# An attention layer over pairs of blocks: correction and factor over the whole width, num a pair further ahead

## The chip, the cores and the metric

The kernel runs on one core of a Trainium2 chip, as one launch. The metric is the device time of one execution in microseconds (us). Engines are named as in the profile: PE is TensorE's matmul, PEld its weight load, DVE is VectorE, ACT is ScalarE, POOL is GpSimd, and SP is SyncE, which here only issues DMAs. L1519 means line 1519 of the kernel before.

## The reference

The input is a matrix x of 2708 rows and 128 columns and a weighted adjacency matrix adj of 2708 by 2708. Four layers follow each other, each one x = layernorm(x + layer(x, adj)). The first is a graph convolution with an adaptive nearest-neighbour term, the third and the fourth are plain graph convolutions. The change lies in the second layer, an attention layer:

```python
XW = jnp.matmul(X, W)
s_col = jnp.matmul(XW, a[0, :f])
s_row = jnp.matmul(XW, a[0, f:])
Z1 = jax.nn.leaky_relu(s_row[:, None] + s_col[None, :], negative_slope=0.01)
den = jnp.exp(Z1)
num = jnp.matmul(A, den)
att = jnp.where(num != 0, den / jnp.where(num != 0, num, 1.0), 0.0)
H = jnp.matmul(A, jnp.matmul(att, XW))
```

So there is one product of 2708 by 2708 by 2708 (num), an elementwise quotient, and two products with narrow matrices.

## The kernel before

The kernel does not compute num as a full product. den(i, j) is exp of a leaky relu of a sum, and so one of two exponentials, according to the sign of s_row(i) + s_col(j). The columns j are sorted by s_col and cut into 44 blocks of 62 (BJ). From one block to the next num changes only by the rows of adj whose sign changes inside the block, at most 126 (KC) of them. So the rows of num for one block are a product of a small weight matrix lw with those gathered rows of adj, plus two rows that carry the sums at the block's beginning. Four blocks (CH) make a chain: the end of one block gives the carried rows of the next.

The steps of the block stage (`block_layer`) are pairs of blocks: 22 pairs (NQ), once for each half h of the columns (HALF = 1354), so 44 steps (h, q). A block takes 64 of the 128 partitions: two rows of carried sums and 62 of num. The 1354 columns are cut into two pieces, "wide" (1024) and "narrow" (330), since num lies in PSUM: the wide piece has two buffers, the narrow one has one, and the sum hacc takes the rest. A step has these parts:

- `load` (L1397, L1403): two gathers of up to 126 rows of adj, issued by POOL, and two copies of the carried rows, issued by SP, into one of three strips of `ring`.
- `find_num` (L1519): the matmuls num <- ring, lw. A piece of 512 or 330 columns has two, one for each block, on 64 columns of PE each, and they show as four records since data are f32.
- `find_inv` (`invert`, L1351 and L1354): ACT's Ln and then Exp(-...) of num, the inverse, in SBUF. For the two carried rows of a block the scale and bias in `plain` make it the inverse of 1.
- `mix_1` (L1361): DVE's err = inverse times num. Its two carried rows are what the next block of the chain needs, and `keep` (L1534) copies them into `carry` with four DMAs from SP where the chain goes on.
- `mix_2` (L1365), here called the correction: a Newton step on the inverse with err. `mix_3` (L1368), here called the factor: the numerator of the quotient, max(gb, g_inv) times the inverse, in place.
- `add_up` (L1376): the matmuls hacc <- inverse, xws, which sum att transposed times XW over the steps of a half.

The order on every engine is written out by hand (`manual_schedule` over all five): what the loop issues first goes first in that engine's queue. Step i of the loop issues the load of step i+2, a fetch of one tile of xws on POOL (L987, the first eight steps), num narrow of i, num wide of i+1, hacc of i-1, the inverses in the same order as the nums, ACT's scaling of xws (L1566, first half only), and then on DVE err, correction and factor of step i, each as wide and narrow. Ahead of the loop stand the loads 0 and 1 and num and inverse of step 0 wide. At the first step of the second half ACT copies the first half's sum (L1568). Behind the last step PE transposes ten tiles (L1587), then does the last hacc. A `POOL` power for the next layer (L253, dinv) and its first loads are queued by their own place in the program. The arm used when a block has more than 126 rows (`dense_layer`) does not run with these inputs.

Of the kernel before, what the change touches and what calls it, by code (L numbers as in the profile page):

```python
# [8 lines left out]
F32 = mybir.dt.float32  # L9
# [43 lines left out]
def kernel(  # L53
# [1294 lines left out]
    def invert(w, num, pool, bufs, sums=True):  # L1348
        inv = pool.tile([P, w], F32, tag=f"inv{w}", name="inv", bufs=bufs)
        if sums:  # L1350
            nc.scalar.activation(inv, num[:, :w], AF.Ln, scale=plain[:, 0:1], bias=plain[:, 1:2])  # L1351
        else:
            nc.scalar.activation(inv, num[:, :w], AF.Ln)
        nc.scalar.activation(inv, inv, AF.Exp, scale=-1.0)  # L1354
        return inv

    def mix_1(w, num, inv, pool):
        err = pool.tile([P, w], F32, tag=f"err{w}", name="err")  # L1360
        nc.vector.tensor_mul(err, inv, num[:, :w])  # L1361
        return err
# [50 lines left out]
    def dense_layer():  # L1413
# [3 lines left out]
        with (  # L1417
# [68 lines left out]
            for h in range(2):  # L1486
                hacc = dps.tile([P, 3 * CW], F32, tag="hacc", name="hacc")
                for q in range(NQ):
# [10 lines left out]
                    inv = invert(HALF, num, dense, 1, sums=False)  # L1499
                    mix_2(inv, mix_1(HALF, num, inv, dense))  # L1500
# [3 lines left out]
    def block_layer():  # L1504
        with (
# [17 lines left out]

            def find_inv(i, piece):
                invs[i, piece] = invert(pieces[piece][1], nums[i, piece], own, 3)

            def keep(i, piece, err):

                (h, q), (c0, w, _) = steps[i], pieces[piece]
                for n in range(2):  # L1530
                    b = block(2 * q + n) + 1
                    if b % CH:
                        o = h * HALF + c0
                        nc.sync.dma_start(  # L1534
                            carry[2 * b : 2 * b + 2, o : o + w], err[n * (BJ + 2) : n * (BJ + 2) + 2, :]
                        )

            def add(i):
# [3 lines left out]
                for piece, (c0, w, _) in pieces.items():  # L1542
                    add_up(w, q, invs[i, piece], haccs[h][:, c0 : c0 + w])

            engines = {nc.tensor, nc.vector, nc.scalar, nc.sync, nc.gpsimd}
            with tc.manual_schedule(engines={e.engine for e in engines}):
                load(0)
                load(1)
                late_q = list(range(SOON, NQ))
                find_num(0, "wide")  # L1550
                find_inv(0, "wide")
                for i, (h, q) in enumerate(steps):
                    if i + 2 < len(steps):
                        load(i + 2)
                    if late_q:
                        fetch_xw(xws, late_q.pop(0))
                    find_num(i, "narrow")
                    if i + 1 < len(steps):
                        find_num(i + 1, "wide")
                    if i:  # L1560
                        add(i - 1)
                    find_inv(i, "narrow")
                    if i + 1 < len(steps):
                        find_inv(i + 1, "wide")
# [4 lines left out]
                    if i + 1 < len(steps):  # L1569
                        errs = {}  # L1570
                        for piece, (c0, w, _) in pieces.items():
                            errs[piece] = mix_1(w, nums[i, piece], invs[i, piece], own)
                            keep(i, piece, errs[piece])
                        for piece in pieces:
                            mix_2(invs[i, piece], errs[piece])
                        for piece, (c0, w, _) in pieces.items():
                            mix_3(w, q, invs[i, piece], h * HALF + c0)
                    else:
                        for piece, (c0, w, _) in pieces.items():
                            mix_2(invs[i, piece], mix_1(w, nums[i, piece], invs[i, piece], own))  # L1580
                            mix_3(w, q, invs[i, piece], h * HALF + c0)
# [133 lines left out]
```

## Time and profile before

| what | us |
|---|---|
| runs of the kernel before: median of 3 | 1096.37 (1093.6 to 1104.44) |
| the profiled execution's own time | 1095.12 |
| its span, first to last instruction | 1093.3 |
| mean granted TensorE clock | 0.968 |

| engine | busy us | share of the span | instructions |
|---|---|---|---|
| PE | 1001.2 | 92% | 3691 |
| DVE | 641.2 | 59% | 1354 |
| ACT | 338.3 | 31% | 617 |
| POOL | 262.2 | 24% | 334 |

The block stage lies between 532 and 763 us of the span. Times in the views are counted from the span's start. In the chain of waits, each entry is what ended last, followed back from the end. In a timeline, a row gives start, time, engine, line, operation, tiles with the buffer numbers left out, and the count of instructions that were merged into it; in brackets stand the idle time ahead of it and what ended that. A matmul's end is modelled, so distances between PE's work are taken from start to start.

### The profile page before, as it was taken

Reading aid. Unit: us, or ns where it says so; the run is one execution under the profiler, and the core shown is the slowest. Engines: PE = TensorE matmul, PEld = TensorE weight load, DVE = VectorE, ACT = ScalarE, POOL = GpSimd, SP = SyncE. Lnnn points to the kernel's source line nnn. Section 1 sums busy time; section 2 is a strip of 40 time slices with the busy share of each in tenths; the row PEclk is TensorE's granted clock in tenths of the full one; section 3 lists DMA queues with packets and bytes.
Section 4 is the critical chain, followed back from the end, with each engine's and each line's share of the span. In section 5 each row is a group of like instructions: output and inputs, shape, how many; then the busy total and the mean of one; then the engine's idle time right before and its main releaser. Section 6 shows DMA issues by size and latency. Waiting matters only on the chain.

```text
span 1093.3 us, 11460 instructions
## 1 busy us (share of the span) xinstructions
PE 1001.2 (92%) x3691; PEld 483.3 (44%) x3691; DVE 641.2 (59%) x1354; ACT 338.3 (31%) x617; POOL 262.2 (24%) x334
## 2 busy tenths in 40 slices
PE   0798999999997898798799999999999999999996
PEld 0345544444443455643233333334444644565444
DVE  5983448999943477772498999998112112132122
ACT  0000125555401144612466776665001100011000
POOL 4000000000565564015584444430112100000000
PEclk9998999999998999699899999999999999999998
DMA  9999330000283556497545545555675875574752
GB/s 341 371 316 279 115 116 1 0 1 1 66 276 119 176 166 202 137 357 244 135 130 161 147 126 161 143 152 181 222 239 150 278 226 185 171 235 159 241 159 76
DMA packets 109380, 190.31 MB, mean 174 GB/s; under 512 B 13666, under 2 KB 46706, under 8 KB 109310
## 3 DMA queue, kind: packets, MB, share of 16 engines
q1 hardware_dynamic: 91408, 151.79, 42.6%
q0 software_dynamic: 17728, 37.62, 12.4%
q8 instruction: 31, 0.51, 0.2%
q14 instruction: 39, 0.32, 0.1%
q10 hardware_dynamic: 174, 0.08, 0.0%
HBM read 214.37 MB, written 4.16 MB: 200 GB/s over the span
## 4 chain that ended last, share of the span: by engine, by line
PE 79%; DVE 7%; DMA 6%; issue 4%; ACT 2%; POOL 1%; another core or an unknown queue 1%; SPq 1%; POOLq 0%; DVEq 0%; ACTq 0%
PE acc L204 32%; PE num L1519 9%; PE hacc L1376 9%; PE acc L647 8%; PE acc L428 7%; DMA res<-in_adjT 3%; PE acc L1270 3%; PE acc L637 2%; DMA got<-y_rows,where 1%; PE mis L285 1%; DVE where L650 1%; DMA part<-in_adjT 1%; DVE near L649 1%; DVE both L483 1%
## 5 line engine op out<-in xcount | busy, mean ns | idle before, releaser
L1397 POOL DMA_INDIRECT ring<-in_adjT,slot_i x88 | 96.2, 1093 | 116.4 <-PE num L1519 87.3
L1519 PE MATMUL num<-ring,lw 128*64 128x512 f32 (+1 forms) x528 | 114.8, 557 | 3.7 <-DVE err L1361 1.9
L1376 PE MATMUL hacc<-inv,xws 128*128 128x512 f32 (+1 forms) x264 | 111.7, 559 | 0.6 <-issue 0.3
L647 PE MATMUL acc<-zT,z 128*128 128x512 f32 (+4 forms) x264 | 108.6, 558 | 0.0
L1351 ACT ACTIVATE inv<-num,plain 128x1024 f32<-128x1024 f32 x88 | 80.6, 916 | 60.6 <-PE num L1519 35.8
L253 POOL TENSOR_TENSOR rstd<-rstd,minus_half 128x4 f32<-128x4 f32 (+1 forms) x18 | 17.3, 960 | 313.4 <-DVE rstd L252 313.4
L648 ACT COPY key<-acc 128x512 f32<-128x512 f32 (+3 forms) x132 | 70.2, 535 | 59.8 <-issue 29.8
L234 ACT COPY gb<-acc 128x512 f32<-128x512 f32 (+2 forms) x18 | 9.6, 535 | 251.0 <-PE acc L204 251.0
L1361 DVE TENSOR_TENSOR err<-inv,num 128x1024 f32<-128x1024 f32 x88 | 74.3, 853 | 20.1 <-ACT inv L1354 16.1
L204 PE MATMUL acc<-ring,y 128*128 128x512 f32 (+2 forms) x192 | 81.3, 554 | 0.5 <-POOL sim L584 0.5
L1376 PEld LDWEIGHTS hacc<-inv,xws 128*128 128x128 f32 x264 | 46.5, 189 | 77.6 <-issue 45.7
L677 POOL DMA_INDIRECT got<-y_rows,where x66 | 69.7, 1056 | 39.1 <-DVE near_sum L690 16.0
L204 PE MATMUL acc<-ring,xs 128*128 128x512 f32 (+2 forms) x192 | 77.2, 545 | 0.0
L1368 DVE SCALAR_TENSOR_TENSOR inv<-gb,g_inv,inv 128x1024 f32<-128x1024 f32 x88 | 77.0, 913 | 0.1
L204 PE MATMUL acc<-ring,carry 128*128 128x512 f32 (+2 forms) x192 | 74.5, 542 | 0.0
L204 PE MATMUL acc<-ring,m_rows 128*128 128x512 f32 (+2 forms) x192 | 74.3, 542 | 0.0
L1365 DVE SCALAR_TENSOR_TENSOR inv<-err,inv 128x1024 f32<-128x1024 f32 x88 | 72.3, 860 | 0.1
L647 PEld LDWEIGHTS acc<-zT,z 128*128 128x128 f32 (+1 forms) x264 | 47.5, 188 | 54.9 <-issue 49.4
L1354 ACT ACTIVATE inv<-inv 128x1024 f32<-128x1024 f32 x88 | 67.6, 768 | 2.8
L649 DVE MAX8 near<-key 128x8 f32<-128x2708 f32 (+1 forms) x22 | 65.5, 2978 | 3.9 <-ACT key L648 3.9
L575 POOL TENSOR_TENSOR slot_e<-near,sim 128x44 f32<-128x44 f32 (+2 forms) x3 | 0.7, 243 | 272.7 <-DVE d2inv L603 266.0
L650 DVE FIND_INDEX8 where<-near,key 128x8 uint32<-128x2708 f32 (+1 forms) x22 | 65.4, 2972 | 0.0
(357 smaller groups left out, 1351.6 us busy)
## 6 DMA issues: line engine op xcount, KB each, us to landing
ring<-in_adjT SPq DMA_DIRECT2D x86, 1024.0 KB
ring<-in_adjT SPq DMA_DIRECT2D x19, 768.0 KB
part<-in_adjT SPq DMA_DIRECT2D x12, 1024.0 KB
ring<-in_adjT SPq DMA_DIRECT2D x19, 552.0 KB
res<-in_adjT SPq DMA_DIRECT2D x4, 1280.0 KB
more<-in_adjT SPq DMA_DIRECT2D x4, 1024.0 KB
part<-in_adjT SPq DMA_DIRECT2D x3, 768.0 KB
part<-in_adjT SPq DMA_DIRECT2D x3, 552.0 KB
```

Source lines behind the costliest of these rows:

```text
L204: nc.tensor.matmul(accs[c][: lhsT.shape[-1], :w], lhsT=lhsT, rhs=src, start=start, stop=stop)
L428: nc.tensor.matmul(accs[c][:, : cw[c]], lhsT=y[:, i, :], rhs=src[:, : cw[c]], start=first, stop=last)
L647: nc.tensor.matmul(pks[c][:p, : cw[c]], lhsT=z2[:, :p], rhs=zT[:, cs], start=False, stop=True)
L649: nc.vector.max(near[:p, t, :], key[:p])
L650: nc.vector.max_index(where[:p, t, :], near[:p, t, :], key[:p])
L1351: nc.scalar.activation(inv, num[:, :w], AF.Ln, scale=plain[:, 0:1], bias=plain[:, 1:2])
L1361: nc.vector.tensor_mul(err, inv, num[:, :w])
L1365: nc.vector.scalar_tensor_tensor(inv, err, 2.0, inv, op0=ALU.subtract, op1=ALU.mult)
L1368: nc.vector.scalar_tensor_tensor(inv, gb[:, col : col + w], g_inv[:, q : q + 1], inv, op0=ALU.max, op1=ALU.mult)
L1376: nc.tensor.matmul(haccs[:, o:e], lhsT=xws[:, q, :], rhs=inv[:, o:e], start=(q == 0), stop=(q == NQ - 1))
L1397: nc.gpsimd.indirect_dma_start(out=rows[i][:KC, n, :], out_offset=None, in_=adj_half[:, :], in_offset=bass.IndirectOffsetOnAxis(ap=slot_i[ ...
L1519: nc.tensor.matmul(num[n * (BJ + 2) : (n + 1) * (BJ + 2), o:e], lhsT=lw[:, 2 * q + n, :], rhs=rows[i][:, n, c0 + o : c0 + e], start=True, ...
```

## The change

- `invert` writes into a tile that it is given. An inverse and an err are now one tile of 1354 columns for both pieces; `part` cuts out a piece.
- The correction and the factor take 1354 columns in one instruction instead of 1024 and 330, but for the last step. err, num and the inverse stay in two pieces.
- The factor of step i-1 is issued with step i, behind err of i and ahead of the correction of i, and hacc of i-1 behind it.
- num and inverse are a step further ahead: step i issues num narrow of i+1 and num wide of i+2, and the load of i+3. Ahead of the loop stand three loads, num and inverse of step 0 and of step 1 wide.
- There are four inverse buffers: three in `own`, and for every fourth step the second half of `mT`, which is free until the end of the stage.
- The copy of the first half's sum stands ahead of the wide inverse of step i+2, and behind the narrow one of i+1.
- Four kept-row DMAs are issued right behind err, ahead of the nums in the program.

The order of the instructions on each engine, as the program is built, is that of the code. On PE a round is num narrow (i+1), num wide (i+2), hacc (i-1); on DVE err wide, err narrow, factor (i-1), correction (i); on ACT inverse narrow (i+1), the scaling of xws, inverse wide (i+2); on SP two row copies of load i+3, four kept-row copies of i; on POOL two gathers of load i+3 and a fetch of xws.

```diff
-    def invert(w, num, pool, bufs, sums=True):
-        inv = pool.tile([P, w], F32, tag=f"inv{w}", name="inv", bufs=bufs)
+    def invert(inv, num, sums=True):
...
-    def mix_1(w, num, inv, pool):
-        err = pool.tile([P, w], F32, tag=f"err{w}", name="err")
-        nc.vector.tensor_mul(err, inv, num[:, :w])
-        return err
...
+            def part(v, piece):
+                c0, w, _ = pieces[piece]
+                return v[:, c0 : c0 + w]
+
             def find_inv(i, piece):
-                invs[i, piece] = invert(pieces[piece][1], nums[i, piece], own, 3)
+                if i not in invs:
+                    invs[i] = mT[:, HALF:] if i % 4 == 1 else own.tile([P, HALF], F32, tag="inv", name="inv", bufs=3)
+                invert(part(invs[i], piece), nums[i, piece])
...
+                end = len(steps)
+                late_q = list(range(SOON, NQ))
                 load(0)
                 load(1)
-                late_q = list(range(SOON, NQ))
-                find_num(0, "wide")
-                find_inv(0, "wide")
+                load(2)
+                for i, piece in ((0, "wide"), (0, "narrow"), (1, "wide")):
+                    find_num(i, piece)
+                    find_inv(i, piece)
                 for i, (h, q) in enumerate(steps):
-                    if i + 2 < len(steps):
-                        load(i + 2)
+                    if i + 3 < end:
+                        load(i + 3)
                     if late_q:
                         fetch_xw(xws, late_q.pop(0))
-                    find_num(i, "narrow")
-                    if i + 1 < len(steps):
-                        find_num(i + 1, "wide")
+                    err = own.tile([P, HALF], F32, tag="err", name="err")
+                    for piece in pieces:
+                        nc.vector.tensor_mul(part(err, piece), part(invs[i], piece), nums[i, piece])
+                        if i + 1 < end:
+                            keep(i, piece, err)
+                    if i + 1 < end:
+                        find_num(i + 1, "narrow")
+                    if i + 2 < end:
+                        find_num(i + 2, "wide")
                     if i:
+                        mix_3(HALF, steps[i - 1][1], invs[i - 1], steps[i - 1][0] * HALF)
                         add(i - 1)
-                    find_inv(i, "narrow")
-                    if i + 1 < len(steps):
-                        find_inv(i + 1, "wide")
+                    if i + 1 < end:
+                        mix_2(invs[i], err)
+                        find_inv(i + 1, "narrow")
                     if h == 0:
                         nc.scalar.mul(xws[:, q, :], xws[:, q, :], g_col[:, q : q + 1])
                     if (h, q) == (1, 0):
                         nc.scalar.copy(mT[:, :HALF], haccs[0][:, :HALF])
-                    if i + 1 < len(steps):
-                        errs = {}
-                        for piece, (c0, w, _) in pieces.items():
-                            errs[piece] = mix_1(w, nums[i, piece], invs[i, piece], own)
-                            keep(i, piece, errs[piece])
-                        for piece in pieces:
-                            mix_2(invs[i, piece], errs[piece])
-                        for piece, (c0, w, _) in pieces.items():
-                            mix_3(w, q, invs[i, piece], h * HALF + c0)
-                    else:
-                        for piece, (c0, w, _) in pieces.items():
-                            mix_2(invs[i, piece], mix_1(w, nums[i, piece], invs[i, piece], own))
-                            mix_3(w, q, invs[i, piece], h * HALF + c0)
+                    if i + 2 < end:
+                        find_inv(i + 2, "wide")
+                for piece, (c0, w, _) in pieces.items():
+                    mix_2(part(invs[end - 1], piece), part(err, piece))
+                    mix_3(w, q, part(invs[end - 1], piece), h * HALF + c0)
```

More of the change, by code (lines that the diff above doesn't have):

```diff
@@ L1346 @@
     more.close()
-    def invert(w, num, pool, bufs, sums=True):
-        inv = pool.tile([P, w], F32, tag=f"inv{w}", name="inv", bufs=bufs)
+    def invert(inv, num, sums=True):
         if sums:
-            nc.scalar.activation(inv, num[:, :w], AF.Ln, scale=plain[:, 0:1], bias=plain[:, 1:2])
+            nc.scalar.activation(inv, num, AF.Ln, scale=plain[:, 0:1], bias=plain[:, 1:2])
         else:
-            nc.scalar.activation(inv, num[:, :w], AF.Ln)
+            nc.scalar.activation(inv, num, AF.Ln)
         nc.scalar.activation(inv, inv, AF.Exp, scale=-1.0)
-        return inv
-    def mix_1(w, num, inv, pool):
-        err = pool.tile([P, w], F32, tag=f"err{w}", name="err")
-        nc.vector.tensor_mul(err, inv, num[:, :w])
-        return err
     def mix_2(inv, err):
@@ L1498, in dense_layer @@
                         nc.scalar.mul(xws[:, q, :], xws[:, q, :], g_col[:, q : q + 1])
-                    inv = invert(HALF, num, dense, 1, sums=False)
-                    mix_2(inv, mix_1(HALF, num, inv, dense))
+                    inv = dense.tile([P, HALF], F32, tag="inv", name="inv")
+                    err = dense.tile([P, HALF], F32, tag="err", name="err")
+                    invert(inv, num[:, :HALF], sums=False)
+                    nc.vector.tensor_mul(err, inv, num[:, :HALF])
+                    mix_2(inv, err)
                     mix_3(HALF, q, inv, h * HALF)
@@ L1534, in keep @@
                         nc.sync.dma_start(
-                            carry[2 * b : 2 * b + 2, o : o + w], err[n * (BJ + 2) : n * (BJ + 2) + 2, :]
+                            carry[2 * b : 2 * b + 2, o : o + w], part(err, piece)[n * (BJ + 2) : n * (BJ + 2) + 2, :]
                         )
@@ L1542, in add @@
                 for piece, (c0, w, _) in pieces.items():
-                    add_up(w, q, invs[i, piece], haccs[h][:, c0 : c0 + w])
+                    add_up(w, q, part(invs[i], piece), haccs[h][:, c0 : c0 + w])
             engines = {nc.tensor, nc.vector, nc.scalar, nc.sync, nc.gpsimd}
             with tc.manual_schedule(engines={e.engine for e in engines}):
+                end = len(steps)
+                late_q = list(range(SOON, NQ))
                 load(0)
                 load(1)
-                late_q = list(range(SOON, NQ))
-                find_num(0, "wide")
-                find_inv(0, "wide")
+                load(2)
+                for i, piece in ((0, "wide"), (0, "narrow"), (1, "wide")):
+                    find_num(i, piece)
+                    find_inv(i, piece)
                 for i, (h, q) in enumerate(steps):
-                    if i + 2 < len(steps):
-                        load(i + 2)
+                    if i + 3 < end:
+                        load(i + 3)
                     if late_q:
                         fetch_xw(xws, late_q.pop(0))
-                    find_num(i, "narrow")
-                    if i + 1 < len(steps):
-                        find_num(i + 1, "wide")
+                    err = own.tile([P, HALF], F32, tag="err", name="err")
[7 more added lines that the diff above has]
+                        find_num(i + 2, "wide")
                     if i:
+                        mix_3(HALF, steps[i - 1][1], invs[i - 1], steps[i - 1][0] * HALF)
                         add(i - 1)
-                    find_inv(i, "narrow")
-                    if i + 1 < len(steps):
-                        find_inv(i + 1, "wide")
+                    if i + 1 < end:
+                        mix_2(invs[i], err)
+                        find_inv(i + 1, "narrow")
                     if h == 0:
```

## The prediction

> **What bounds the kernel now.** I read the page first (which engine carries the chain), then busy time by stage, then the chain inside the block stage, then the timelines of TensorE (PE), VectorE (DVE), ScalarE (ACT) and GpSimd (POOL) there. The change touches only the block stage, which runs from PE's first num product at 532.6 us to its last hacc product, which ends at 758.1 us.
>
> ```profile
> 600.00:650.00 50.00, 50.00 (x186) 18.62 (x184) 49.65 (x62) 37.59 (x52) 21.69 (x21) 1.00 0.50 136
> ```
>
> This is a row of busy time by stretch: length, then PE, weight loads, DVE, ACT, POOL, the granted clock and the DMA share. PE and DVE are both full, so busy time cannot say which of them sets the pace. The chain can:
>
> ```profile
> by line: PE hacc L1376 50.3%; PE num L1519 50.0%
> ...
> 604.15 2.43 PE num L1519 x12
> 606.58 2.47 PE hacc L1376 x6
> 609.05 2.43 PE num L1519 x12
> ```
>
> From 580 to 740 us the chain never leaves PE: twelve num matmuls in 2.43 us and six hacc matmuls in 2.47 us, 4.90 us a step. DVE follows it closely:
>
> ```profile
> 604.86 1.74 DVE L1361 TENSOR_TENSOR err<-inv,num 128x1024 f32<-128x1024 f32 x2
> ...
> 605.59 0.48 ACT L1354 ACTIVATE inv<-inv 128x330 f32<-128x330 f32 x1
> ...
> 606.51 1.65 DVE L1365 SCALAR_TENSOR_TENSOR inv<-err,inv 128x1024 f32<-128x1024 f32 x2
> ...
> 608.09 1.75 DVE L1368 SCALAR_TENSOR_TENSOR inv<-gb,g_inv,inv 128x1024 f32<-128x1024 f32 x2
> ...
> 609.76 1.74 DVE L1361 TENSOR_TENSOR err<-inv,num 128x1024 f32<-128x1024 f32 x2
> ```
>
> Each row is a pair of instructions, 1024 and 330 wide: start, time from the first start to the last end. DVE's period is 609.76-604.86 = 4.90 us. The groups by form give single durations:
>
> ```profile
> L1365 DVE SCALAR_TENSOR_TENSOR inv<-err,inv 128x1024 f32<-128x1024 f32 x25 | 30.8, 1231 | 0.0
> L1368 DVE SCALAR_TENSOR_TENSOR inv<-gb,g_inv,inv 128x1024 f32<-128x1024 f32 x24 | 30.6, 1273 | 0.0
> L1361 DVE TENSOR_TENSOR err<-inv,num 128x1024 f32<-128x1024 f32 x25 | 30.2, 1208 | 0.8 <-issue 0.8
> ...
> L1368 DVE SCALAR_TENSOR_TENSOR inv<-gb,g_inv,inv 128x330 f32<-128x330 f32 x24 | 13.2, 550 | 0.0
> ...
> L1365 DVE SCALAR_TENSOR_TENSOR inv<-err,inv 128x330 f32<-128x330 f32 x24 | 11.8, 491 | 0.0
> ```
>
> The pairs of L1365 and L1368 overlap by 0.07 us (1.231+0.491-1.65; 1.273+0.550-1.75). The err pair has a gap of 0.03 us instead (the 330 form takes 0.498 us), because the narrow err waits for ACT's narrow inverse, which ends at 605.59+0.48 = 606.07, as the wide err does (604.86+1.21). So DVE itself needs about 4.80 us; the last 0.10 us is PE's pace, handed on through ACT. The time that is not PE at its pace lies at the start:
>
> ```profile
> 532.60 5.94 PE L1519 MATMUL num<-ring,lw 128*64 128x512 f32 x20 [0.52 <-ACT carry L1282]
> 540.42 2.50 PE L1519 MATMUL num<-ring,lw 128*64 128x330 f32 x12 [1.88 <-DVE err L1361]
> 543.26 2.51 PE L1376 MATMUL hacc<-inv,xws 128*128 128x512 f32 x6 [0.34 <-issue]
> 545.70 0.78 PE L1519 MATMUL num<-ring,lw 128*64 128x330 f32 x4
> 547.29 2.10 PE L1519 MATMUL num<-ring,lw 128*64 128x512 f32 x8 [0.81 <-DMA ring<-carry]
> 549.32 2.54 PE L1376 MATMUL hacc<-inv,xws 128*128 128x512 f32 x6
> ...
> 566.47 3.61 PE L1519 MATMUL num<-ring,lw 128*64 128x330 f32 x12
> ```
>
> Start to next start, num took 3.62 us at 545.70, 3.54 at 566.47, and by the same timeline 3.95 at 572.48 and 3.13 at 578.90, instead of 2.43: 4.5 us over. The first 32 matmuls (532.60 to 543.26, 10.66 us) would take 6.6 at pace: 4.1 over. So 8.6 us is all that any reordering of the waits can win here. The last three of those waits are for gathered rows, and POOL shows why:
>
> ```profile
> 557.10 4.03 POOL L253 TENSOR_TENSOR dinv<-dinv,minus_half 128x22 f32<-128x22 f32 x1
> 561.35 1.75 POOL L1397 DMA_INDIRECT ring<-in_adjT,slot_i  x1 [0.22 <-PE hacc L1376]
> 563.41 1.06 POOL L1397 DMA_INDIRECT ring<-in_adjT,slot_i  x1 [0.30 <-issue]
> ```
>
> A power of 4.03 us stands in POOL's queue ahead of the gathers for step 7, so PE goes on only at 568.15, 4.7 us after the second gather's issue.
>
> **The change part by part.**
>
> *Wider correction and factor.* From the rows the slope of L1365 is (1231-491)/694 = 1.07 ns a column, so 1354 columns take 0.491+1024x0.00107 = 1.58 us where the pair took 1.65; L1368 takes 0.550+1024x0.00104 = 1.62 where the pair took 1.75. That saves 0.07+0.13 = 0.20 us a step; DVE needs 4.60. PE still needs 4.90, with the same 18 matmuls in the same num-hacc alternation, so this is worth 0. Cover: PE's 0.10 us lead becomes 0.30. [...]
>
> *Correction and factor a pair apart.* DVE's order becomes err(i) wide and narrow, factor(i-1), correction(i). hacc(i-1) now waits for a factor one position later, but hacc keeps its place in a round. With T the start of num narrow(i+1) on PE: ACT's narrow inverse (0.08 us after the 0.85 us of matmuls, then 0.63+0.48) ends at T+2.1, err narrow(i+1) at T+2.6, factor(i) at T+4.1; hacc(i) is due at T+4.9+2.4 = T+7.3. The next num narrow is due at T+4.9 and its buffer is free at T+2.6. ACT does 0.63+0.48+1.21+1.06+0.39 = 3.8 us a step. No loop is near 4.90: cost 0. The new wait of err wide on the four kept-row copies of step i-2 is covered too: SP's six transfers take 3.7 us a step, and err(i) is two steps later.
>
> *num a pair further ahead.* A load has two gathers on POOL and two row copies on SP. A ring of three strips still frees a strip after num narrow(j-3) and needs it at num wide(j), two rounds (9.6 us) later, as before. On POOL the order load, fetch, load, fetch between step 3 and step 10 stays (fetch numbers shift by one), and the power stays ahead of load 7. On SP load(j) passes one kept-row group (4 transfers, 2.45 us), so the row-copy wait of 0.81 us at 547.29 goes; what follows it there is the DVE chain. But num wide(i+2) now stands in PE's queue ahead of hacc(i-1), with one hacc (2.47 us) less done. At the start: DVE puts correction(0), 1.58 us, ahead of err(1), so num narrow(2) starts near 543.6 instead of 545.7, with no hacc done instead of one. POOL's waits for num at 546.76 (0.92 us) and 552.85 (0.53 us) go; with its other durations (2.02 and 1.89 us there) kept, load 7 comes 0.85 us earlier, and so do loads 8 and 9, behind which PE waits again. PE thus passes num wide(9) 0.85 us earlier but owes 2.47 us more hacc: 2.47-0.85 = +1.6 us. Ends: -4.5 us (all four late rounds repaired) and +3.5 (loads not earlier at all, and 1 us more for load 10). I take +1.6, since the same POOL rows set it.
>
> *The copy at the middle.* ACT's copy of hacc (1.29 us in the groups) now stands ahead of the wide inverse of two steps on. It waits for hacc(21), at T+4.9, ends at T+6.3; the wide inverse ends at T+8.6, the narrow one at T+9.75, err narrow at T+10.3, and num narrow, due at T+9.8, is late: +0.6 us (0 to 1.3).
>
> *The end.* Before, from the last num narrow (750.95) to 758.09 is 7.14 us. Now two haccs and the transposes (1.52) and the last hacc follow it: hacc(41) to 3.2, hacc(42) waits for factor(42) until 4.1, then 6.5, transposes to 8.0, hacc(43) to 10.45. One hacc more is owed there: 10.45-7.14-2.47 = +0.8 us (0 to 2.5, one whole hacc).
>
> *Four inverse buffers.* The buffer of inverse i+2 was last read by hacc(i-2), a round earlier: 0.
>
> **Sum:** 0+0+1.6+0.6+0.8 = +3.0 us on the profiled execution's 1095.1 us (span 1093.3) = 1098.1. The median of the runs shown is 1096.4, 1.3 us above the profiled one, so I say 1098.5. The runs spread from 1093.6 to 1104.4; a difference under 1% can hardly be told from none.
>
> **Rivals.**
> 1. *The late start is repaired* (chance 0.14). If the gathers come earlier than POOL's rows suggest, up to 8.6 us goes, less the 1.4 us of middle and end: about 1089. For: the row-copy wait does go. Against: the 4.03 us power keeps its place.
> 2. *DVE was the bound* (0.06). Then a step falls from 4.90 to 4.60, over about 40 steps -12 us: 1083 to 1087. For: DVE is 99% busy. Against: the err gap behind ACT, and a chain without DVE. [...]
> 3. *Gathers become late in every round* (0.08). Place: num wide(i+2), with hacc(i-1) queued behind it. In the steady stretch a pair needs 0.3+1.35+4.7 = 6.4 us of the 9.6; it decides when landing takes 3.2 us more. The landing at 580.17, 7.2 us after an issue at 572.96, is the worst seen. At 0.3 us a round: +12+3 us, 1110.
>
> **How the numbers follow.** The forecast has 0.72, about 1093 to 1104. Of the rivals, 2 ends beyond -1% (below 1085.4) with most of its chance, 3 beyond +1% (above 1107.3). Faster 0.05, same 0.87, slower 0.08. Leaving out some 2 in 10, the range reaches into rival 1 and to the edge of rival 3: 1088 to 1107.
>
> **What would show it.** Right: rounds of 2.43+2.47 us in the steady stretch with DVE idle near 0.3 us a step; gather waits again near 564 to 580 us, with hacc behind them; one PE wait of half a microsecond near the middle; hacc(42) waiting at the end. Wrong: rounds shorter than 4.90 (rival 2), no gather waits (rival 1), or waits in every round (rival 3).

## The result and the profile after

Measured side by side, the kernel before took 1098.37 us and the changed one 1101.07 us (medians of 22 runs each): a ratio of 1.0041, 95% interval 1.0022 to 1.0061. That is +4.5 us, between +2.4 and +6.7, by the ratio on record; the two medians alone lie 2.7 us apart. The forecast was +3.0 us and "the same". The profiled execution of the changed kernel took 1101.07 us, with a span of 1099.3; the one before had 1093.3. So the two traces differ by 6.0 us.

The steady rounds first. This is the row of busy time by stretch that answers to the one in the prediction (length, PE, weight loads, DVE, ACT, POOL, granted clock, DMA share, GB/s):

```profile
600.00:650.00 50.00, 50.00 (x188) 18.81 (x190) 47.61 (x42) 36.90 (x51) 21.03 (x21) 1.00 0.51 138
```

DVE fell from 49.65 to 47.61 us of 50 and from 62 instructions to 42, while PE stayed full. The groups by form between 600 and 700 us give the new instructions (count, busy us, mean ns):

```profile
L1356 DVE SCALAR_TENSOR_TENSOR inv<-err,inv 128x1354 f32<-128x1354 f32 x16 | 25.0, 1561 | 0.0
L1359 DVE SCALAR_TENSOR_TENSOR inv<-gb,g_inv,inv 128x1354 f32<-128x1354 f32 x15 | 24.3, 1622 | 0.0
```

1.56 and 1.62 us, where 1.58 and 1.62 had been worked out. From there on the round is 2.43 + 2.47 us on PE, as before. The loss lies at the start. TensorE's timeline of the changed kernel, from the third round:

```profile
542.98 2.50 PE L1513 MATMUL num<-ring,lw 128*64 128x330 f32 x12 [0.67 <-issue]
545.40 2.54 PE L1367 MATMUL hacc<-inv,xws 128*128 128x512 f32 x6
547.87 2.50 PE L1513 MATMUL num<-ring,lw 128*64 128x330 f32 x12
...
562.56 0.78 PE L1513 MATMUL num<-ring,lw 128*64 128x330 f32 x4
564.17 1.07 PE L1513 MATMUL num<-ring,lw 128*64 128x512 f32 x2 [0.83 <-DMA ring<-in_adjT,slot_i]
566.26 1.93 PE L1513 MATMUL num<-ring,lw 128*64 128x512 f32 x6 [1.02 <-DMA ring<-in_adjT,slot_i]
568.12 2.54 PE L1367 MATMUL hacc<-inv,xws 128*128 128x512 f32 x6
570.59 1.63 PE L1513 MATMUL num<-ring,lw 128*64 128x330 f32 x6
573.68 1.93 PE L1513 MATMUL num<-ring,lw 128*64 128x512 f32 x6 [1.46 <-DMA ring<-in_adjT,slot_i]
575.55 2.54 PE L1367 MATMUL hacc<-m_rows,xws 128*128 128x512 f32 x6
578.02 3.58 PE L1513 MATMUL num<-ring,lw 128*64 128x330 f32 x12
581.53 2.54 PE L1367 MATMUL hacc<-inv,xws 128*128 128x512 f32 x6
584.00 3.69 PE L1513 MATMUL num<-ring,lw 128*64 128x330 f32 x12
587.63 2.54 PE L1367 MATMUL hacc<-inv,xws 128*128 128x512 f32 x6
```

Read it from start to start. num of a round should take 2.43 us; it takes 568.12-562.56 = 5.56, then 4.96, 3.51 and 3.63: 7.9 us over in four rounds, all waiting for gathered rows, with hacc behind them in the queue. Before, three such rounds were 3.3 us over, and a fourth waited 1.2 us for a row copy; that one is gone. POOL's timeline shows the gathers (L1388) and fetches (L987):

```profile
555.07 4.30 POOL L253 TENSOR_TENSOR dinv<-dinv,minus_half 128x22 f32<-128x22 f32 x1
559.59 1.55 POOL L1388 DMA_INDIRECT ring<-in_adjT,slot_i  x1 [0.22 <-issue]
561.45 1.06 POOL L1388 DMA_INDIRECT ring<-in_adjT,slot_i  x1 [0.30 <-issue]
562.81 2.82 POOL L987 DMA_INDIRECT xws<-xw_rows,row_j  x1 [0.30 <-issue]
565.94 1.04 POOL L1388 DMA_INDIRECT ring<-in_adjT,slot_i  x1 [0.30 <-issue]
567.29 2.93 POOL L1388 DMA_INDIRECT ring<-in_adjT,slot_i  x1 [0.30 <-issue]
570.52 1.03 POOL L987 DMA_INDIRECT xws<-xw_rows,row_j  x1 [0.30 <-issue]
571.86 1.04 POOL L1388 DMA_INDIRECT ring<-in_adjT,slot_i  x1 [0.30 <-issue]
573.21 2.37 POOL L1388 DMA_INDIRECT ring<-in_adjT,slot_i  x1 [0.30 <-issue]
```

The power and load 7 start some 2 us earlier than before (561.45 against 563.41 for load 7's second gather); 0.71 us of that is the stage itself, which starts earlier by so much in this trace (531.89 against 532.60). But then one fetch and two gathers take 2.82, 2.93 and 2.37 us instead of 1.05. Load 8's second gather is 1.30 us earlier than before (567.29 against 568.59), load 9's is 0.25 us later (573.21 against 572.96) and load 10's 1.32 us later (578.68 against 577.36). Counted from the first num of the stage, load 7 is 1.25 us earlier, load 8 0.59 earlier, load 9 0.96 later and load 10 2.03 later; and since the second gathers of loads 8 and 9 also take longer, they end 1.29 and 2.28 us later than before (570.22 against 569.64, 575.58 against 574.01 in the traces' times). DVE's timeline of the same stretch shows what they ran beside:

```profile
561.63 1.62 DVE L1359 SCALAR_TENSOR_TENSOR inv<-gb,g_inv,inv 128x1354 f32<-128x1354 f32 x1
563.17 1.56 DVE L1356 SCALAR_TENSOR_TENSOR m_rows<-err,m_rows 128x1354 f32<-128x1354 f32 x1
564.65 1.62 DVE L1562 TENSOR_TENSOR err<-inv,num 128x1024 f32<-128x1024 f32 x2
566.19 1.62 DVE L1359 SCALAR_TENSOR_TENSOR m_rows<-gb,g_inv,m_rows 128x1354 f32<-128x1354 f32 x1
567.73 1.56 DVE L1356 SCALAR_TENSOR_TENSOR inv<-err,inv 128x1354 f32<-128x1354 f32 x1
```

The fetch that starts at 562.81, inside a factor, ends at 565.63, which is 0.90 us after the end of the correction behind it (564.73). The gather of 567.29, also inside a factor, ends at 570.22, 0.93 us after the correction's end (569.29). The gather of 565.94, beside an err, takes 1.04.

I add up by stretches. Distances are taken from PE's starts, from the first num of the stage; the column "to step 12" ends at num narrow of step 12, where the kernel before has done one hacc (2.47 us) more.

| trace | to step 12 | 12 to 20 | 20 to 30 | 30 to 43 | 43 to the next layer | stage |
|---|---|---|---|---|---|---|
| before | 66.58 | 39.16 | 48.96 | 63.64 | 9.01 | 227.36 |
| after | 68.00 | 39.17 | 49.37 | 63.65 | 12.04 | 232.24 |

In both traces the stage begins with the clock at 0.50, for its first 3.37 us before and 4.24 us after; num narrow of step 1 starts 7.82 and 7.92 us into the stage, so that this hardly divides the two.

The start loses 68.00+2.47-66.58 = 3.9 us, the middle 0.41, the end 12.04-9.01-2.47 = 0.56: together 4.9. The other 1.1 us is about the balance of what lies outside the stage: 0.7 us won ahead of it (its first num starts at 531.89 instead of 532.60), and 1.7 lost right behind it. There the changed kernel's trace has this row, by stretch:

```profile
764.83:768.24 3.41, 3.41 (x9) 1.77 (x8) 2.43 (x10) 0.00 (x0) 0.00 (x0) 0.50 0.01 2
```

For 3.41 us TensorE was granted half its clock, at 3.41 x 0.5 = 1.7 us lost. From the start at 764.13 PE's first 16 matmuls behind the stage take 4.77 us here, and 3.08 in the control of group C (736.30 to 739.38), whose clock stays at 1.00: 1.69 us apart. The trace of before has no such drop there.

The middle, where ACT copies the first half's sum. ACT of the changed kernel:

```profile
658.75 1.29 ACT L1578 COPY m_rows<-hacc 128x1354 f32<-128x1354 f32 x1 [3.02 <-PE hacc L1367]
659.94 1.21 ACT L1350 ACTIVATE inv<-num,plain 128x1024 f32<-128x1024 f32 x1
```

and PE's answer, one round later:

```profile
663.96 2.50 PE L1513 MATMUL num<-ring,lw 128*64 128x330 f32 x12 [0.34 <-DVE err L1562]
```

The copy waits for hacc, the wide inverse behind it is late, err narrow too, and num starts 0.41 us behind its pace. The end of the stage, on PE:

```profile
752.09 0.78 PE L1513 MATMUL num<-ring,lw 128*64 128x330 f32 x4
752.79 2.54 PE L1367 MATMUL hacc<-m_rows,xws 128*128 128x512 f32 x6
756.29 2.51 PE L1367 MATMUL hacc<-inv,xws 128*128 128x512 f32 x6 [0.96 <-DVE inv L1359]
758.64 1.26 PE L1589 MATMUL pt<-ident,m_rows 128*128 128x128 f32 x10
759.73 2.44 PE L1367 MATMUL hacc<-inv,xws 128*128 128x512 f32 x6
764.13 0.77 PE L1606 MATMUL mis<-ident,m_rows 128*128 128x128 f32 x5 [1.96 <-ACT m_rows L160]
```

hacc(42) waits 0.96 us for its factor, as forecast.

### The profile page after: what moved, and what is told of

It is laid out like the page before. It is cut to its first block, busy times and chain, and to the rows that moved or that the text cites. A ratio compares the mean times of both kernels' runs of the same rounds, so it can differ in the third digit from the quotient of the medians.

```text
span 1099.3 us, 11350 instructions
## 1 busy us (share of the span) xinstructions
PE 1007.4 (92%) x3691; PEld 485.1 (44%) x3691; DVE 632.4 (58%) x1268; ACT 337.6 (31%) x617; POOL 267.4 (24%) x334
## 4 chain that ended last, share of the span: by engine, by line
PE 77%; DVE 6%; DMA 5%; issue 4%; ACT 3%; another core or an unknown queue 2%; POOL 2%; SPq 0%; POOLq 0%; ACTq 0%; DVEq 0%
PE acc L204 32%; PE num L1513 9%; PE acc L647 8%; PE hacc L1367 8%; PE acc L428 7%; DMA res<-in_adjT 3%; PE acc L637 2%; PE acc L1270 2%; PE mis L285 1%; DVE where L650 1%; DMA got<-y_rows,where 1%; DVE near L649 1%; DMA part<-in_adjT 1%; DVE both L483 1%
## 5 line engine op out<-in xcount | busy, mean ns | idle before, releaser
L1388 POOL DMA_INDIRECT ring<-in_adjT,slot_i x88 | 100.5, 1142 | 111.9 <-PE num L1513 82.7
L1367 PE MATMUL hacc<-inv,xws 128*128 128x512 f32 (+1 forms) x198 | 83.7, 559 | 1.0 <-DVE inv L1359 1.0
L1350 ACT ACTIVATE inv<-num,plain 128x1024 f32<-128x1024 f32 x66 | 60.4, 915 | 48.3 <-PE num L1513 46.1
L1562 DVE TENSOR_TENSOR err<-inv,num 128x1024 f32<-128x1024 f32 x66 | 55.7, 855 | 29.6 <-ACT inv L1353 25.0
L1513 PEld LDWEIGHTS num<-ring,lw 128*64 128x64 f32 x528 | 36.1, 138 | 69.7 <-issue 46.5
L1367 PEld LDWEIGHTS hacc<-inv,xws 128*128 128x128 f32 x198 | 34.9, 189 | 58.2 <-issue 46.3
L428 PE MATMUL acc<-part,y 128*128 128x512 f32 (+2 forms) x120 | 52.8, 601 | 5.3 <-DMA part<-in_adjT 3.1
L1359 DVE SCALAR_TENSOR_TENSOR inv<-gb,g_inv,inv 128x1354 f32<-128x1354 f32 (+2 forms) x34 | 53.8, 1582 | 0.1
```

Of the source, the lines that this page charges most:

```text
L428: nc.tensor.matmul(accs[c][:, : cw[c]], lhsT=y[:, i, :], rhs=src[:, : cw[c]], start=first, stop=last)
L1350: nc.scalar.activation(inv, num, AF.Ln, scale=plain[:, 0:1], bias=plain[:, 1:2])
L1367: nc.tensor.matmul(haccs[:, o:e], lhsT=xws[:, q, :], rhs=inv[:, o:e], start=(q == 0), stop=(q == NQ - 1))
L1388: nc.gpsimd.indirect_dma_start(out=rows[i][:KC, n, :], out_offset=None, in_=adj_half[:, :], in_offset=bass.IndirectOffsetOnAxis(ap=slot_i[ ...
L1513: nc.tensor.matmul(num[n * (BJ + 2) : (n + 1) * (BJ + 2), o:e], lhsT=lw[:, 2 * q + n, :], rhs=rows[i][:, n, c0 + o : c0 + e], start=True, ...
L1562: nc.vector.tensor_mul(part(err, piece), part(invs[i], piece), nums[i, piece])
```

## The experiments

The runs come in three groups; the kernels of a group ran on one chip together with the kernel before. That kernel took 1066.74 us in group A, 1100.45 in group B and 1064.21 in group C, so a time is compared inside its group only, as a ratio to it, with the 95% interval in brackets. For traces, the control in group C (the changed kernel again) is also the nearest one for group A, and the first trace of the changed kernel (the one shown above) for group B. The granted clock speaks for this choice: in the traces of the kernel before, of the changed kernel (the first) and of all of group B it is 0.50 for the first 3.2 to 4.6 us of the stage, and num narrow of step 0 starts 3.3 to 3.4 us after the first num; in the traces of groups A and C it is 1.00 there, and that distance is 1.74 us. One of these has a half clock a little later, a_power, from 507.87 to 511.28 us.

In each experiment, the theory at the time was: the late rounds at the start come from POOL's power and from hacc queued behind a late num; the middle and the end are separate small losses; DVE paces nothing.

### Group A: the power moved, and the width by itself

**a_power**, the changed kernel with POOL's power ahead of the block stage, in the phase before it:

```diff
+            inv_sqrt_of(dinv, deg, DEG_EPS, True)
...
-        inv_sqrt_of(dinv, deg, DEG_EPS)
```

> The changed kernel, with POOL's 4 us power for the next layer computed before the block stage, where POOL idles. Theory (the power in POOL's queue makes the gathers of steps 7 to 10 late, and the change pays more for it because one hacc more waits behind num): of the four late num rounds between 562 and 588 us, which are 3.1, 2.5, 1.1 and 1.2 us over their 2.43 us, at least three quarters goes, 6 us or more, and the time comes out about 0.3% under the kernel before. Rival (the gathers are late by the rate of the transfers, the power only happens to stand there): more than half of the 7.9 us stays, and the time stays above the kernel before.

**b_power**, the same on the kernel before.

> The kernel before with the same power moved out of the block stage. Theory: its three late rounds (1.1, 1.5 and 0.7 us over) go, the row-copy wait of 1.2 us at 547 stays, and it gains about 3 us, 0.3%; that is less than the same edit brings to the changed kernel. Rival (rate of the transfers): the late rounds stay and the gain is under 1 us.

Measured: a_power 0.9981 [0.9954, 1.0007], b_power 0.9965 [0.9938, 0.9992]. In a_power's trace no round is late any more. Its POOL timeline from the fifth step on:

```profile
522.94 1.20 POOL L1389 DMA_INDIRECT ring<-in_adjT,slot_i  x1 [0.30 <-issue]
524.43 1.05 POOL L1389 DMA_INDIRECT ring<-in_adjT,slot_i  x1 [0.30 <-issue]
525.79 1.40 POOL L987 DMA_INDIRECT xws<-xw_rows,row_j  x1 [0.30 <-issue]
527.50 1.20 POOL L1389 DMA_INDIRECT ring<-in_adjT,slot_i  x1 [0.30 <-issue]
```

A load and a fetch take POOL 527.50-522.94 = 4.56 us of PE's 4.90. That explains why one power of 4.3 us costs so much: POOL has 0.34 us a round to spare and cannot catch up while the fetches last. The stage takes 223.45 us with the change and 222.45 without, against 229.37 in the control. The difference of 1.0 us between the two is the middle (0.41) and the end (0.55); at the start the changed order is level (59.22+2.47 = 61.69 against 61.67). In fact it is ahead there, for a_power's trace holds the half clock named above: its num narrow of step 2 starts 10.30 us into the stage, where it is 9.42 in a_best (group C), which has the same order up to there and the full clock. So with POOL ahead, the hacc owed is won back in full, and some 0.8 us more; nearly all of the loss at the start needs the power in POOL's queue.

**a_split**, the changed kernel with correction and factor in two pieces again, order kept:

```diff
-                        mix_3(HALF, steps[i - 1][1], invs[i - 1], steps[i - 1][0] * HALF)
+                        for piece, (c0, w, _) in pieces.items():
+                            mix_3(w, steps[i - 1][1], part(invs[i - 1], piece), steps[i - 1][0] * HALF + c0)
...
-                        mix_2(invs[i], err)
+                        for piece in pieces:
+                            mix_2(part(invs[i], piece), part(err, piece))
```

> The changed kernel with correction and factor taken back to two instructions each, 1024 and 330 wide; everything else stays. Theory (PE paces the steady stretch): rounds stay 2.43 + 2.47 us, DVE's idle of 0.25 us a step ahead of the narrow err shrinks to about 0.1, and the time is that of the changed kernel within 1.5 us. Rival (DVE paces it): rounds of 5.1 us and 8 us more.

**b_wide**, the kernel before with one tile for both pieces of the inverse and of err, and `mix_2` and `mix_3` over 1354 columns; its order is kept.

> The kernel before with correction and factor over 1354 columns in one instruction each, the order of the steps unchanged. Theory (PE paces): rounds stay 4.90 us and the time is that of the kernel before within 1.5 us; the last step may move by a few tenths. Rival (DVE paces): rounds of 4.70 us and 8 us less. Second rival (a correction that follows its narrow err directly stalls): rounds over 4.90 us and a loss.

Measured: a_split 1.0010 [0.9981, 1.0039], b_wide 1.0007 [0.9975, 1.0039]. The steady rounds are 4.90 us in both (39.17 and 39.16 us for eight). DVE's width paces nothing there: rival 2 is out, and DVE's 99% was no bound. But in a_split the rounds to step 12 take 62.87 us, where the control takes 65.13. Its POOL timeline behind the power:

```profile
533.05 1.06 POOL L1388 DMA_INDIRECT ring<-in_adjT,slot_i  x1 [0.30 <-issue]
534.42 1.03 POOL L987 DMA_INDIRECT xws<-xw_rows,row_j  x1 [0.30 <-issue]
535.75 1.70 POOL L1388 DMA_INDIRECT ring<-in_adjT,slot_i  x1 [0.30 <-issue]
537.76 1.05 POOL L1388 DMA_INDIRECT ring<-in_adjT,slot_i  x1 [0.30 <-issue]
```

No instruction there is above 1.75 us, and the loads come every 537.76-533.05 = 4.71 us. In the first trace of the changed kernel they come 567.29-561.45 = 5.84 and 5.92 us apart, and in the control 5.85 and 5.91: slower than PE's 4.90. (Before they came 5.18 and 4.37 us apart.) This had not been expected. In all fourteen traces, the stage holds 1265 DMA instructions on POOL. 305 of them took over 1.10 us. Each of the 305 started while DVE was in a correction or factor, and each ended 0.87 to 0.98 us after the end of one. No instruction outside such a stretch, beside err or with DVE idle, took over 1.10; nor did 33 that started in the first 0.01 or the last 0.2 us of one. Where POOL's instruction comes into two such DVE instructions of 1.6 us that follow each other at once, it can be held through both: 2.8 to 2.9 us (562.81 and 567.29 above). What in the hardware holds it no run shows. That narrower pieces let it in more often is not shown: from 637.92 us on, in the steady rounds, five gathers of a_split took 2.30 to 2.86 us, and b_wide, with wide instructions in the order of before, has none above 2.07 and takes 52.97 us from step 2 to step 12, where before takes 53.49. What is shown is when an instruction is held; how often that happens depends on how POOL's instructions fall against DVE's. What goes over 1.05 us adds up, in the first 57 us of the stage, to 5.6 us before, 7.6 after, 8.1 in the control and 4.5 in a_split.

### Group B: the middle, the end, and hacc ahead of num

**a_tail**, the changed kernel with the transposes of `mT` ahead of the last but one hacc:

```diff
+                        if i + 1 == end:
+                            turn_early()
                         add(i - 1)
```

> The changed kernel with the ten transposes of the stage's end put ahead of the last but one hacc, so that PE has work while that hacc's factor is made. Theory: PE's wait of 0.96 us for the factor goes, and with it the drop of the granted clock to 0.5 for 3.4 us that follows 2.5 us later and costs 1.7 us: 2.0 to 2.7 us less than the changed kernel. Rival (the drop has nothing to do with that wait): the wait goes but the drop stays, 0.5 to 1 us less.

Measured: 1.0015 [0.9981, 1.0048]; the last stretch takes 10.98 us instead of 12.04, and the half clock behind the stage isn't there; the runs do not tell it from the changed kernel. The 1.06 us is about the wait (0.96) that the transposes now fill. The expectation tied the half clock to that wait, but in the changed kernel's first trace it came 8.5 us behind it. Just ahead of it stood another, of 1.96 us (764.13); in a_tail this one is 1.87 us.

**a_copy**, the changed kernel with the copy of the first half's sum behind the wide inverse:

```diff
-                    if (h, q) == (1, 0):
-                        nc.scalar.copy(mT[:, :HALF], haccs[0][:, :HALF])
                     if i + 2 < end:
                         find_inv(i + 2, "wide")
+                    if (h, q) == (1, 0):
+                        nc.scalar.copy(mT[:, :HALF], haccs[0][:, :HALF])
```

> The changed kernel with the copy of the first half's sum put behind the wide inverse of two steps on instead of ahead of it. Theory: DVE's wait of 2.98 us for that inverse near 662 us shrinks below 0.5 us and PE's lost 0.44 us there goes; nothing else moves, so the time is about 0.4 us lower, which only the trace can show. Rival: the loss moves to the next hacc, which needs the copy's buffer, and the sum stays.

Measured: 1.0072 [1.0042, 1.0101]. The loss at the middle is gone in the trace (48.96 us from step 20 to 30, as before), but the time isn't lower; its interval overlaps that of the changed kernel, so a loss isn't shown either. ACT waits 5.1 us for num, 19.3 us into the stage; a_first has 4.8 us at that place and the first trace of the changed kernel 2.4. I could not find what sets it, and it stays open. It doesn't explain the time, since the stage of this trace is shorter than that of the changed kernel (229.54 against 232.24).

**a_first**, the changed kernel with hacc(i-1) ahead of num wide(i+2) on PE, in every round:

```diff
-                    if i + 2 < end:
-                        find_num(i + 2, "wide")
                     if i:
...
                         add(i - 1)
+                    if i + 2 < end:
+                        find_num(i + 2, "wide")
```

> The changed kernel with hacc of i-1 ahead of num wide of i+2 on PE, so that a late gather no longer holds a hacc up. Theory: the four late rounds lose about the 2.47 us of one hacc in all, since hacc runs while the gather lands; but the wide inverse is now later by a hacc, so that the factor of i-1 ends at about the time at which hacc wants it: 0 to 0.3 us more in each steady round, 0 to 12 us in all. Rival (the queue order does not matter, the gathers alone set the start): the start does not get shorter.

Measured: 1.0098 [1.0067, 1.0129]. The first twelve rounds shorten to 66.55 us, but the steady rounds lengthen, from 39.17 to 40.39 us for eight. PE's timeline there:

```profile
644.06 2.51 PE L1367 MATMUL hacc<-m_rows,xws 128*128 128x512 f32 x6
646.50 2.50 PE L1513 MATMUL num<-ring,lw 128*64 128x512 f32 x12
649.24 2.51 PE L1367 MATMUL hacc<-inv,xws 128*128 128x512 f32 x6 [0.25 <-DVE inv L1359]
```

hacc waits for the factor every second round: in this order the factor is due one num wide earlier, and the path through ACT's inverse and DVE sets the pace (DVE itself waits 0.26 to 0.54 us for ACT ahead of err). Two stretches of half clock also lie in this trace, 566.11 to 569.53 and 770.91 to 774.33, each worth an estimated 1.7 us (3.41 x 0.5): without the first, the twelve rounds would take about 64.8 us. "A pair apart" is free only behind num wide.

**a_all**, the last three and the power together:

> The changed kernel with four edits: the power before the stage, hacc ahead of num wide, the copy behind the wide inverse, the transposes ahead of the last but one hacc. Theory: the start's late rounds, the middle's 0.4 us and the end's 2.4 us go; if the steady rounds stay at 4.90 us it is 8 to 10 us under the changed kernel, some 5 us under the kernel before; if hacc waits 0.2 us for the factor in every round, it is about level with the kernel before.

Measured: 1.0140 [1.0101, 1.0178]; the theory missed. It keeps a_first's long rounds, and near 655 us there is a new wait, since hacc of the second half needs the buffer that the copy empties, the copy stands behind a wide inverse, and that one's num now stands behind hacc:

```profile
655.62 2.50 PE L1514 MATMUL num<-ring,lw 128*64 128x512 f32 x12
661.15 3.70 PE L1368 MATMUL hacc<-inv,xws 128*128 128x512 f32 x6 [3.04 <-ACT m_rows L1593]
```

### Group C: a control, and the parts that held

**a_again**, the changed kernel as it is.

> The changed kernel as it is, on the chip of the next three runs, so that they can be compared with it. Both theories: 1.004 of the kernel before (1.002 to 1.006), the stage from the first num to the next layer's first product 232.2 us, four late rounds, some 8 us over. The drop of the granted clock to 0.5 for 3.41 us behind the stage, which was in some traces of this order and not in others: if it belongs to the order it is here again, if it is chance it may be missing, with the stage's time unchanged and the 4.8 us behind it down to about 3.1.

Measured: 1.0028 [1.0004, 1.0053], stage 229.37 us. Three rounds are over by 6.8 us. The wait at the end is the same, and the clock stays at 1.00 behind it: the half clock doesn't follow from the order alone. What the traces show of it is in the last section.

**a_early**, hacc ahead of num wide in the rounds i = 3 to 8 alone, the power left in place:

```diff
+                    early = 3 <= i <= 8
-                    if i + 2 < end:
+                    if i + 2 < end and not early:
                         find_num(i + 2, "wide")
...
                         add(i - 1)
+                    if early:
+                        find_num(i + 2, "wide")
```

> The changed kernel with hacc ahead of num wide in the six rounds i = 3 to 8 alone, where the loads come late; the power stays where it is. Theory (a late num wide keeps a hacc waiting behind it): the first twelve rounds are as short as where hacc stood ahead in every round, 66.55 instead of 68.00 us, and the steady rounds stay at 2.43 + 2.47 (39.17 us for eight), since the 0.15 us a round that the other order cost there isn't paid; stage 230.8 us, 1.4 under the changed kernel. Rival (the loads alone set these rounds, whatever stands behind): 68.0 us and 232.2, no difference.

Measured: 0.9992 [0.9970, 1.0014], stage 226.55 us, 2.8 under the control, all of it before step 12 (62.31 against 65.13); steady rounds 39.17. The expectation's level of 66.55 was that of another chip; its difference of 1.4 us came out twice as large, and the 1.7 us of half clock in a_first's first rounds are about what it lacked. That fits a late num wide that holds up a hacc. How much of the 2.8 is that, and how much is that POOL's instructions fell differently against DVE's (its longest is 2.40 us), the run can't tell: counted from the first num, the last gathers of loads 8 and 9 are issued by 33.87 and 38.75 us, 2.1 and 2.5 us ahead of the control, though what goes over 1.05 us in the first 57 us adds up to 7.4 us, against 8.1 there.

**a_best**, the power, the copy and the turning moved, num wide left ahead of hacc:

> The changed kernel with the power ahead of the stage, the copy of the first sums behind the wide inverse, and the turning ahead of the last but one hacc. If the three losses are separate, as the theory has it, they add: 232.24 - 8.8 (late rounds) - 0.41 (middle) - 1.06 (end) = 222.0 us of stage, against 222.45 in the kernel before with the power moved: level with that kernel or 0.5 us under it, about 0.996 to 0.997 of the kernel before. Rival: the pieces take it from one another (as the copy did where hacc stood ahead of num, which gave a wait of 9 us near the middle): the stage is then over 224 us.

**b_power2**, the kernel before with the power moved, again:

> The kernel before with the power ahead of the stage, again, as what the best form of the change has to beat: 0.9965 of the kernel before (0.994 to 0.999), stage 222.5 us. Under both theories the same; if the form of the change above is over 1.5 us faster than this, the change has a worth of its own that none of the theories has.

Measured: a_best 0.9944 [0.9925, 0.9964], b_power2 0.9969 [0.9950, 0.9989]. The stage takes 221.16 and 222.40 us; here the small losses do add up as separate ones. a_best is faster than both kernels, by 0.6% and (0.9944 / 1.0028) about 0.8%. Against b_power2 it is 1.24 us shorter in the stage: 0.50 at the end and 0.76 at the start. In group A the same comparison of the start gave nothing (61.69 against 61.67), but there a_power's half clock hid 0.8 us. The gain lies at step 2, whose num waits for a row copy in b_power2 and takes 3.55 us, and 2.43 in a_best. Set against each other directly, the twelve runs of each give 0.9974 (about 0.9956 to 0.9992, an estimate from their means and spread). So with its losses repaired the change is worth about 0.3% on this chip; how much of that is the order itself and how much the moved transposes was not tried apart. The expectation's 222.0 us was 0.8 too long because it used a_power's start, half clock included (59.22 against 58.39); and the wait of 9 us that its rival names isn't in a_all's trace, where PE waits 3.04 us. The end of a_best:

```profile
714.89 2.54 PE L1368 MATMUL hacc<-m_rows,xws 128*128 128x512 f32 x6
717.27 1.25 PE L1552 MATMUL pt<-ident,m_rows 128*128 128x128 f32 x10
718.39 4.90 PE L1368 MATMUL hacc<-inv,xws 128*128 128x512 f32 x12
```

hacc(41), the transposes, then two haccs without a wait: the factor of step 42 is ready by then.

| trace | to step 12 | 12 to 20 | 20 to 30 | 43 to the next layer | stage | ratio to before |
|---|---|---|---|---|---|---|
| a_power (A) | 59.22 | 39.17 | 49.37 | 12.03 | 223.45 | 0.9981 |
| b_power (A) | 61.67 | 39.16 | 48.96 | 9.01 | 222.45 | 0.9965 |
| a_split (A) | 62.87 | 39.17 | 49.37 | 11.63 | 226.69 | 1.0010 |
| b_wide (A) | 64.95 | 39.16 | 48.96 | 9.07 | 225.78 | 1.0007 |
| a_tail (B) | 67.40 | 39.17 | 49.37 | 10.98 | 230.58 | 1.0015 |
| a_copy (B) | 65.71 | 39.17 | 48.96 | 12.05 | 229.54 | 1.0072 |
| a_first (B) | 66.55 | 40.39 | 50.46 | 15.42 | 238.57 | 1.0098 |
| a_all (B) | 63.89 | 40.39 | 54.93 | 12.66 | 237.57 | 1.0140 |
| a_again (C) | 65.13 | 39.17 | 49.37 | 12.04 | 229.37 | 1.0028 |
| a_early (C) | 62.31 | 39.17 | 49.37 | 12.04 | 226.55 | 0.9992 |
| a_best (C) | 58.39 | 39.17 | 48.96 | 10.98 | 221.16 | 0.9944 |
| b_power2 (C) | 61.62 | 39.17 | 48.95 | 9.01 | 222.40 | 0.9969 |

In the kernels with the order of before (b_), "to step 12" holds one hacc of 2.47 us more, and the last stretch one less. The stretch 20 to 30 of a_all, and the first and the last one of a_first, hold a further 3.41 us of half clock each.

## Why the prediction was right, and where it was not

- *Wider correction and factor, 0.* Right for PE's rounds: DVE's instructions took 1.56 and 1.62 us, the steady rounds stayed, and a_split and b_wide confirm it. What it left out shows at the start. The step looked for what hides DVE's time and not for who waits for DVE: POOL's DMA instructions do, and there a fetch and two gathers were held to 2.4 to 2.9 us. How much of that the width causes is not shown: with the pieces narrow again (a_split) the start was 2.3 us shorter in one trace, but with wide ones in the old order (b_wide) nothing was lost, in one trace too. The trace of before had this too: the gather of 561.35 took 1.75 us and the fetch of 564.77 took 1.83, where undisturbed ones took 1.05. I had used those times without asking what set them.
- *A pair apart, 0.* Right in this order; a_first (40.39 us for eight steady rounds instead of 39.17) shows that it hangs on hacc standing behind num wide.
- *num a pair further ahead, +1.6.* The term that was mis-sized: 3.9 us in the first trace. The near step was right (num narrow of step 2 started 11.09 us into the stage, where the forecast's 543.6 makes 11.0; the row-copy wait went). What failed is "with its other durations kept, load 7 comes 0.85 us earlier, and so do loads 8 and 9": the durations were not kept. Counted from the first num, load 7 came 1.25 us earlier and load 8 0.59 earlier, but load 8's last gather was held, load 9 came 0.96 later and load 10 2.03 later, and four rounds were late instead of three. The upper end, +3.5, named this case and fell 0.4 short. The hacc owed is real, yet not a loss by itself: a_power wins it back. The 8.6 us that a reordering could win at most was too high: its 4.1 us for the first 32 matmuls hold 3.37 us at half clock, 1.7 us that no order of the waits gives back.
- *The copy, +0.6:* 0.41. *The end, +0.8:* 0.56, with hacc(42) waiting where it was expected and 10.08 us (752.09 to 759.73+2.44) where 10.45 was worked out. *Four buffers, 0:* nothing in the traces waits for one.
- *Not foreseen:* the half clock behind the stage, 1.7 us in the first trace of the changed kernel and none in the control. The sum of the forecast lacked about 2.3 us at the start, had 0.4 too many at the middle and the end, and lacked 1.1 outside the stage: 3.0+2.3-0.4+1.1 = 6.0, the difference of the traces. That the total still lies in the range owes something to luck: 1088 to 1107 is 19 us wide, much more than the effect, and the term for the start missed by more than it was worth (2.3 on 1.6). By the runs it is 4.5 us, and on the chip of the control 3.0 (0.4 to 5.6).
- *The rivals.* Rival 1, the start repaired, takes the power out of the way: the change alone doesn't do it. Rival 2 fell. Rival 3, late gathers in every round, did not come: past step 12 POOL has no fetches and waits for PE (2.50 us ahead of a load at 600.96, 605.85 and 610.75 in the changed kernel's first trace).

What stays open: whether the wide instructions' hold on POOL or the queue on PE is the larger part of the loss at the start. a_split and a_early each took 2.3 and 2.8 us off it in single traces. The two were not tried together, and nothing tells whether it is the width of DVE's instructions or only how POOL's fall against them.

## What to carry to other kernels

POOL's queue, 93% busy here (4.56 of 4.90 us), could not absorb a single 4.3 us instruction; in a queue that full, move such a one first: by itself it was worth 0.3%, where the reordering cost as much. An instruction's duration in a trace can hold a wait: where the same DMA instruction takes 1.05 us in one place and 1.8 in another, look at what the other engines ran at that time before carrying the number over to a new order. An engine with time to spare (DVE: 47.61 us busy of 50) can still hold up another: here every POOL DMA instruction over 1.10 us ended 0.87 to 0.98 us after the end of one of DVE's. Ask who waits for an engine before making its instructions longer.

## What the runs showed of the hardware

- POOL's DMA instructions took 1.02 to 1.07 us beside DVE's err, which reads one operand from PSUM, or beside an idle DVE; all 305 long ones started at a correction or factor, which read both tensors from SBUF, and ended 0.87 to 0.98 us after one, the longest at 2.93 us. Whether it is the operation or the place of its operands that matters, no run tells apart.
- In each of the fourteen traces the granted TensorE clock is 0.50 or 1.00, and all its changes lie a whole multiple of 3.41 us apart. Behind the stage PE waits 1.95 or 1.96 us for ACT in the seven traces that have the changed order and its transposes in their old place. Where this wait lay whole between two marks of that grid (the changed kernel's first: 762.17 to 764.13, marks at 761.41 and 764.83; likewise a_copy and a_first), the clock fell to 0.50 at the second mark, for 3.41 us. Where a mark cut it (a_power, a_split, a_early and the control), it stayed at 1.00. In the other seven traces the wait is 1.87 us, and it lay whole between two marks in four of them without a fall. So in the traces with 1.95 or 1.96 us the place of the wait told the falls from the others; idle time alone did not, for in a_first a fall at 566.11 followed two waits that sum to 1.88 us. What makes the clock fall no run shows.
